# Layer 0 of a four-layer kernel: the softplus of delta moved from VectorE to TensorE and ScalarE

## The chip, the cores and the metric

The kernel runs on one core of a Trainium2 chip, in one launch, all in fp32. The metric is the device time of one execution in microseconds (us). Engines: TensorE (PE; its weight loads are PEld) multiplies matrices into PSUM; VectorE (DVE), ScalarE (ACT) and GpSimd (POOL) work on tiles; SyncE (SP) issues most transfers. Each runs its own instructions in order and waits for the others by semaphores.

## The reference

Input `x` has shape (4, 64, 64, 128): four images of 4096 tokens with 128 channels. Four layers follow one another; the change is in layer 0, a two-dimensional selective scan. Cut to what matters:

```python
xz = x @ w_in                              # x: group-normed; 2 * 256 channels
xc, z = split(xz)
xa = silu(depthwise_conv3x3(xc) + conv_b)
dts, Bp, Cp = split(xa @ w_xproj)          # 8 + 16 + 16
dts = dts @ w_dt                           # 256 channels
delta = softplus(dts + b_dt)
# four scans over the tokens: rows, columns, and both backwards
h = h * exp(delta * A) + (delta * u) * B   # 16 states per channel
y = sum_n(h * C) + u * D
y = layer_norm(y_rows + y_cols + y_rows_back + y_cols_back) * silu(z)
x = x + y @ w_out
```

Layers 1 to 3 (a recurrence in the Fourier domain, an attention with a mixture of experts, and a windowed attention with another) are not touched.

## The kernel before, in words

**The main loop of layer 0** (line 974 on) runs over 512 iterations I: four images b, two halves h of the 256 channels, 64 chunks c of 64 tokens. An iteration has two *half-steps* (kp = 0 and 1). In each, `products` (L850) multiplies on TensorE into two PSUM tiles `db`; VectorE adds the carry (L865) and runs two scans of 128x1024 (L870); GpSimd makes the next carry (L877) and multiplies the result by C (L885); `total` (L905) sums the states of the chunk two iterations earlier on TensorE into `yp`. After the second part of `total`, ScalarE copies `yp` out (L919); there is one `yp`, so the next iteration's `total` waits for these copies. After the first scans of an iteration VectorE makes `du` (L826). ScalarE also computes the *decay* exp(delta * A) of the next four chunks (a quad), four activations per iteration (`decay`, L773), into one of two buffers.

`db` has three buffers of which a half-step takes two. So the first matmuls of the next `products` may run at once, but the rest wait until the first of the two running scans has ended: TensorE can be about half a half-step ahead of VectorE.

**Work beside the loop.** While image b is scanned, the generators `back` of image b - 1, and `front` and `middle` of image b + 1 are advanced at fixed places: one *slot* after `total` in each half-step (lines 1013 and 1026; one more in some iterations with h = 0). A generator runs to its next `yield`, and so its instructions stand in a written order on TensorE, VectorE and ScalarE (`manual_schedule`). Between half-steps TensorE's order is: `products`, `total`, slot work, `products` again. All slot work of these generators shares one PSUM bank, `bg` (`own_bank`, one buffer), so a tile there is released only when its last reader is done.

`middle` prepares the scan's inputs, in eight blocks k of 512 tokens, in the half h = 1 of the image before. It is used for images 1 to 3; image 0 goes through `opening`, which the change leaves alone. One block is a *round* of 14 slots, seven iterations:

- slots 0 to 3: for each half the convolution (L383, 24 instructions), Silu, a transposition (`columns`, L393) and its copy
- slot 4: `projected` (L404) and two copies; slot 5: `turned_b` (L418) and a copy by VectorE
- slot 6: for half 0, `steps` (L426, the product with `w_dt` into `bg`), then ScalarE: Abs (L491), Relu (L492), Exp (L493), Identity with bias 1 (L494), Ln (L496)
- slot 7: for half 0, VectorE sums (L498, L501, L502), and the result is stored (`keep_steps`, L432)
- slots 8 and 9: the same two for half 1
- slots 10 to 13: for each half `columns` and `flipped` (L435), each with a copy (L516) and a store

With u = exp(-|s|) for s = dts + b_dt, and w the rounded 1 + u, softplus is ln(w) - ((w - 1) - u) + relu(s); the middle term gives back what the rounding of 1 + u took. Even slots lie in the first half-step of an iteration, and the decay of that iteration follows them on ScalarE; the `yp` copies come behind the decay. ScalarE's Ln and Exp each need a table load (L496, L773), which the profile shows as ACT_TABLE_LOAD.

The tiles u, r, v and the other 2 KB tiles of the generators come from one pool of ten buffers (`tmp`, "t2k").

Of the kernel before, what the change touches and what calls it, by code (L numbers as in the profile page):

```python
# [8 lines left out]
AF = mybir.ActivationFunctionType  # L9
ALU = mybir.AluOpType  # L10
# [4 lines left out]
P = 128  # L15
# [5 lines left out]
BLK = 512  # L21
# [39 lines left out]
def tl(pool, shape, tag, dtype=F32, bufs=None):  # L61
    return pool.tile(shape, dtype, name=tag, tag=tag, bufs=bufs)
# [99 lines left out]
def layer0(cm, x, W, x1, also, ahead, kept):  # L162


    tc, nc = cm.tc, cm.nc
    wl = kept.enter_context(tc.tile_pool(name="l0k", bufs=1))
    dr = kept.enter_context(tc.tile_pool(name="l0dram", bufs=2, space=DRAM))
    with ExitStack() as ctx:
        ctx.enter_context(nc.allow_non_contiguous_dma(reason="parameters laid over partitions"))
        wp = ctx.enter_context(tc.tile_pool(name="l0w", bufs=1))  # L170
        tmp = ctx.enter_context(tc.tile_pool(name="l0t", bufs=10))
# [66 lines left out]
        for i in range(2):  # L238
            t = tl(wp, [P, QC, 2, NH0, TC], f"dA{i}")
# [16 lines left out]
        for i in range(2):  # L256
            t = tl(wp, [P, 8, PADW], f"padded{i}")
# [108 lines left out]
        def shifted(i, pool, tag, queue=nc.sync):  # L366

            k, h = divmod(i, 2)
            x3 = [tl(pool, [3 * CG, 2, 8 * PADW], tag) for _ in range(2)]
            for dy in range(3):  # L370
                s0 = (8 * k + dy) * PADW
                for i in range(2):
                    queue.dma_start(
                        x3[i][dy * CG : (dy + 1) * CG],
                        xc_d[4 * h + 2 * i : 4 * h + 2 * i + 2, :, s0 : s0 + 8 * PADW]
                        .rearrange("g p s -> p g s"),
                    )
            return x3

        def convolved(ps, h, x3):  # L380
            for dx in range(3):
                for g in range(4):
                    nc.tensor.matmul(  # L383
                        ps[g * CG : (g + 1) * CG, :], lhsT=cdiag[:, 4 * h + g, dx, :],
                        rhs=x3[g // 2][:, g % 2, :].rearrange(
                            "p (r w) -> p r w", w=PADW
                        )[:, :, dx : dx + HW],
                        start=(dx == 0), stop=(dx == 2),
                    )

        def columns(ps, src):
            for i in range(4):
                nc.tensor.transpose(  # L393
                    ps[:, i * P : (i + 1) * P], src[:, i * P : (i + 1) * P], cm.ident
                )

        def keep_turned(b, h, k, t):
            nc.sync.dma_start(
                img[b]["xT"][h, k * BLK : (k + 1) * BLK, :].rearrange("(t p) c -> p t c", p=P), t
            )  # L400

        def projected(ps, xa):
            for h in range(2):
                nc.tensor.matmul(  # L404
                    ps[0:NX, :], lhsT=w_xp[:, h, :], rhs=xa[h], start=(h == 0), stop=(h == 1)
                )

        def keep_c(b, k, xd):
            nc.sync.dma_start(
                img[b]["ct"][8 * k : 8 * k + 8].rearrange("c n t -> n c t"),  # L410
                xd[RANK + NST : NX, :].rearrange("n (c t) -> n c t", t=TC),
            )

        def turned_b(ps, k, xd, xr):
            pb = ps[:, 0 : 8 * NST].rearrange("p (c n) -> p c n", n=NST)
            for c in range(8):
                for j in range(2):
                    nc.tensor.matmul(  # L418
                        pb[j * TC : (j + 1) * TC, c, :],
                        lhsT=xr[0:NX, c, :] if j else xd[0:NX, c * TC : (c + 1) * TC],  # L420
                        rhs=cm.ident[0:NX, RANK : RANK + NST], start=True, stop=True,
                    )
            nc.vector.tensor_copy(BT[:, 8 * k : 8 * k + 8, :], pb)

        def steps(ps, h, xd):
            nc.tensor.matmul(  # L426
                ps, lhsT=w_dt[:, h * P : (h + 1) * P], rhs=xd[0:RANK, :],
                start=True, stop=True,
            )

        def keep_steps(b, h, k, r):
            nc.sync.dma_start(img[b]["dl"][h, :, k * BLK : (k + 1) * BLK], r)  # L432

        def flipped(ps, t):
            nc.tensor.matmul(  # L435
                ps, lhsT=flip, rhs=t.rearrange("p t c -> p (t c)"), start=True, stop=True
            )

        def keep_both(b, h, k, j, t):
            for i in range(2):  # L440
                nc.sync.dma_start(
                    img[b]["dT"][h, 8 * k + i : 8 * k + 8 : 2, j]
                    .rearrange("t r c -> r t c"), t[i * TC : (i + 1) * TC],
                )

        def middle(b, bank, pool, tag, ahead):

            ready = [shifted(i, pool, tag) for i in range(ahead)]
            for k in range(NBLK):
                cols = slice(k * BLK, (k + 1) * BLK)  # L450
                xa = []
                for h in range(2):
                    ps = bank()
                    convolved(ps, h, ready.pop(0))
                    if 2 * k + h + ahead < 2 * NBLK:
                        ready.append(shifted(2 * k + h + ahead, pool, tag))
                    xh = tl(tmp, [P, BLK], "t2k")
                    nc.scalar.activation(xh, ps, AF.Silu, bias=vec[:, 0, h : h + 1])
                    y0 = tl(tmp, [P, BLK], "t2k")
                    nc.scalar.activation(y0, xh, AF.Copy, scale=d4[:, h : h + 1])  # L460
                    nc.sync.dma_start(img[b]["y0"][:, h, cols], y0)
                    xa.append(xh)
                    yield
                    ps = bank()
                    columns(ps, xa[h])
                    t = tl(tmp, [P, 4, P], "t2k")
                    nc.scalar.copy(t, ps.rearrange("p (t c) -> p t c", c=P))
                    keep_turned(b, h, k, t)
                    yield
                ps = bank()  # L470
                projected(ps, xa)
                xd = tl(tmp, [P, BLK], "t2k")
                nc.scalar.copy(xd[0:NX, :], ps[0:NX, :])
                xr = tl(tmp, [P, 8, TC], "t2k")
                nc.scalar.copy(
                    xr[0:NX], ps[0:NX, :].rearrange("p (c t) -> p c t", t=TC)[:, :, ::-1]
                )
                keep_c(b, k, xd)
                yield
                turned_b(bank(), k, xd, xr)  # L480
                rs = []
                for h in range(2):
                    yield


                    ps = bank()
                    steps(ps, h, xd)
                    bias = vec[:, 1, h : h + 1]
                    u = tl(tmp, [P, BLK], "t2k")
                    r = tl(tmp, [P, BLK], "t2k")  # L490
                    nc.scalar.activation(u, ps, AF.Abs, bias=bias)  # L491
                    nc.scalar.activation(r, ps, AF.Relu, bias=bias)  # L492
                    nc.scalar.activation(u, u, AF.Exp, scale=-1.0)  # L493
                    nc.scalar.activation(ps, u, AF.Identity, bias=cm.ones[:, 0:1])  # L494
                    v = tl(tmp, [P, BLK], "t2k")
                    nc.scalar.activation(v, ps, AF.Ln)  # L496
                    yield
                    nc.vector.scalar_tensor_tensor(  # L498
                        ps, ps, 1.0, u, ALU.subtract, ALU.subtract
                    )  # L500
                    nc.vector.tensor_tensor(ps, v, ps, ALU.subtract)  # L501
                    nc.vector.tensor_tensor(r, ps, r, ALU.add)  # L502
                    keep_steps(b, h, k, r)
                    rs.append(r)

                yield
                for h in range(2):
                    t = None
                    for j in range(2):
                        ps = bank()  # L510
                        if j == 0:
                            columns(ps, rs[h])
                        else:
                            flipped(ps, t)
                        t = tl(tmp, [P, 4, P], "t2k")
                        nc.scalar.copy(t, ps.rearrange("p (t c) -> p t c", c=P))  # L516
                        keep_both(b, h, k, j, t)
                        yield
# [215 lines left out]
        def place(I):  # L734
            u, c = divmod(I, NCHUNK)
            return divmod(u, 2) + (c,)
# [237 lines left out]
        with tc.manual_schedule(engines=engines):  # L974
            for I in range(N):
                b, h, c = place(I)
# [19 lines left out]
                w = quads.get(I // QC + 1)  # L996
# [1829 lines left out]
```

## Time and profile before

| what | us |
|---|---|
| runs shown: lowest, median, highest | 10,066.63, 10,080.76, 10,089.57 |
| the profiled execution's own time | 10,065.04 |
| its span, first to last instruction | 10,063.1 |
| main loop of layer 0, about 219 to 5,653 us of the span | 5,434 |
| busy in the span: PE, DVE, ACT, POOL | 8,590.0, 7,471.3, 5,347.1, 5,373.5 |
| of it the scans L870 | 4,571.0 |
| of it GpSimd's product L885 | 4,659.0 |
| three VectorE lines of the softplus in `middle`, 48 times each | 99.0 |

In the profile's lines a group is: line, engine, operation, out<-in with the shapes, xcount, then busy time in us and the mean of one instruction in ns, then the idle time before it and who ended it. Lines of a timeline have the start in us from the span's first instruction, the length, the engine and the line; what stands in brackets is the engine's idle time before, and its releaser. A table by stage gives for each stretch its length, each engine's busy time and number of instructions, the clock granted to TensorE (1.00 is full), the busy share of the DMA engines and GB/s.

### The profile page before, as it was taken

How to read it: one execution, taken by the hardware profiler on the slowest of the kernel's cores; microseconds unless marked ns; L12 is line 12 of the kernel's file. 1: busy time of each engine (PE TensorE's matmuls, PEld its weight loads, DVE VectorE, ACT ScalarE, POOL GpSimd, SP SyncE). 2: the span in 40 equal slices, each digit the busy share in tenths (PEclk: the TensorE clock that was granted, in tenths of full speed). 3: DMA queues.
4: the chain of work that ended last, by engine and by line, in shares of the span. 5: the costliest groups of instructions: out<-in, count | busy, mean ns of one | idle time of the engine just before them, and what ended most of it. 6: DMA issues, size and time to landing. Idle time of an engine off the chain costs nothing.

```text
span 10063.1 us, 193320 instructions
## 1 busy us (share of the span) xinstructions
PE 8590.0 (85%) x73048; PEld 4219.2 (42%) x73048; DVE 7471.3 (74%) x11089; ACT 5347.1 (53%) x13309; POOL 5373.5 (53%) x2788
## 2 busy tenths in 40 slices
PE   7888888889988899988888649999999958888776
PEld 3333444444434444444333334444444435554442
DVE  4999999999999999999999765454551123455656
ACT  5775555775547665556522237767776613443331
POOL 4999999899999899999999500000000000100000
PEclk8899999999999999999999869999999977888887
DMA  7344454445543455444333321111101062212101
GB/s 212 103 132 128 137 141 114 128 130 146 145 126 120 120 160 144 132 120 124 87 103 94 107 66 31 37 38 34 38 18 33 16 223 48 61 45 52 43 24 47
DMA packets 1081627, 957.38 MB, mean 95 GB/s; under 512 B 165356, under 2 KB 825616, under 8 KB 1073920
## 3 DMA queue, kind: packets, MB, share of 16 engines
q1 hardware_dynamic: 1055298, 880.82, 29.7%
q0 software_dynamic: 18560, 63.37, 3.4%
q8 instruction: 586, 9.60, 0.4%
q14 instruction: 337, 2.76, 0.1%
q10 hardware_dynamic: 6846, 0.83, 0.1%
HBM read 608.77 MB, written 335.80 MB: 94 GB/s over the span
## 4 chain that ended last, share of the span: by engine, by line
PE 42%; DVE 26%; POOL 10%; issue 8%; ACT 6%; DMA 5%; SPq 2%; DVEq 0%; ACTq 0%; POOLq 0%
DVE big L870 15%; POOL big L885 8%; PE qk L1758 7%; PE av L1817 7%; PE yp L905 5%; PE db L850 4%; PE x L2607 2%; DVE tex L2613 2%; DVE du L826 2%; PE s L2373 1%; DMA xo<-xT_d 1%; PE po L2398 1%; PE bg L383 1%; DVE mx L2337 1%; PE s L2331 1%
## 5 line engine op out<-in xcount | busy, mean ns | idle before, releaser
L885 POOL TENSOR_TENSOR big<-big,ct 128x2048 f32<-128x2048 f32 x1024 | 4659.0, 4550 | 76.1
L870 DVE TENSOR_TENSOR_SCAN big<-dA,db 128x1024 f32<-128x1024 f32 x2048 | 4571.0, 2273 | 13.6 <-DMA xo<-xT_d 8.6
L850 PE MATMUL db<-dg,du 32*64 32x256 f32 x32768 | 1896.0, 418 | 606.0 <-DVE big L870 466.6
L905 PE MATMUL yp<-big,both 128*64 128x256 f32 x16384 | 2229.3, 419 | 60.5 <-ACT yc L919 47.6
L905 PEld LDWEIGHTS yp<-big,both 128*64 128x64 f32 x16384 | 1191.8, 148 | 1031.0 <-issue 563.6
L850 PEld LDWEIGHTS db<-dg,du 32*64 32x64 f32 x32768 | 653.3, 135 | 1791.9 <-issue 1692.3
L1817 PE MATMUL av<-e,x 128*128 128x512 f32 x2048 | 974.0, 592 | 4.6 <-ACT e L1812 4.6
L1762 ACT ACTIVATE e<-qk,nk 128x512 f32<-128x512 f32 x1024 | 692.6, 685 | 534.1 <-PE qk L1758 533.2
L1758 PE MATMUL qk<-a,xT 128*128 128x512 f32 x2048 | 966.6, 594 | 8.6 <-ACT e L1762 7.9
L919 ACT COPY yr<-yp 128x64 f32<-128x64 f32 x1024 | 221.7, 216 | 1346.9 <-PE yp L905 1331.4
L818 ACT ACTIVATE dg<-mask,BT 128x32 f32<-128x32 f32 x4096 | 896.6, 318 | 10.9 <-PE db L850 8.6
L773 ACT ACTIVATE dA<-dp,A 128x252 f32<-128x252 f32 x2048 | 866.0, 498 | 49.8 <-issue 26.1
L1331 POOL TENSOR_TENSOR g_rs<-g_rs,k_qrow 128x4 f32<-128x4 f32 x32 | 41.0, 1282 | 1499.9 <-DVE g_rs L1330 1499.9
L1758 PEld LDWEIGHTS qk<-a,xT 128*128 128x128 f32 x2048 | 378.0, 190 | 462.3 <-issue 358.0
L1817 PEld LDWEIGHTS av<-e,x 128*128 128x128 f32 x2048 | 381.6, 190 | 434.7 <-issue 393.2
L1812 ACT ACTIVATE e<-e 128x1024 f32<-128x1024 f32 x510 | 538.7, 1056 | 15.4
L877 POOL TENSOR_TENSOR cy<-big,a 128x32 f32<-128x32 f32 x1008 | 365.6, 363 | 299.6 <-DVE big L870 239.3
L2380 ACT ACTIVATE e<-s 128x576 f32<-128x576 f32 x448 | 272.7, 647 | 398.8 <-PE s L2373 396.2
L2112 POOL TENSOR_TENSOR ln_rs<-ln_rs,mroot 128x4 f32<-128x4 f32 x64 | 64.8, 1012 | 756.0 <-DVE ln_rs L2111 501.6
L2392 POOL COPY vp<-vt 112x80 f32<-112x80 f32 x112 | 30.2, 270 | 781.2 <-PE po L2398 755.3
L2613 DVE SCALAR_TENSOR_TENSOR tex<-x,gw,tex 128x128 f32<-128x128 f32 x768 | 264.5, 344 | 198.0 <-PE x L2607 184.3
L826 DVE TENSOR_TENSOR du<-xo,dt 128x256 f32<-128x256 f32 x512 | 387.7, 757 | 0.0
(569 smaller groups left out, 9805.6 us busy)
## 6 DMA issues: line engine op xcount, KB each, us to landing
ct<-ct_d SPq DMA_DIRECT2D x1024, 128.0 KB
xo<-xT_d SPq DMA_DIRECT2D x2048, 32.0 KB
dg_d<-dg SPq DMA_DIRECT2D x256, 256.0 KB
dg<-dg_d SPq DMA_DIRECT2D x256, 256.0 KB
t4k<-xc_d SPq DMA_DIRECT2D x288, 132.0 KB
dp<-dl_d SPq DMA_DIRECT2D x256, 128.0 KB
dT_d<-t2k SPq DMA_DIRECT2D x256, 128.0 KB
dt<-dT_d SPq DMA_DIRECT2D x512, 64.0 KB
```

The costliest lines, as they stand in the source:

```text
L773: nc.scalar.activation(w["dA"][:, :, g, n, 1:], w["dp"][:, g, :, 1:], AF.Exp, scale=A[:, w["h"], g, n : n + 1],)
L818: nc.scalar.activation(q["dg"][:, n, :], mask, AF.Copy, scale=BT[:, q["c"], n : n + 1])
L826: nc.vector.tensor_tensor(q["du"], q["xo"], q["dt"].unsqueeze(1).to_broadcast([P, 2, P]), ALU.mult)
L850: nc.tensor.matmul(bs[j][p * TC : (p + 1) * TC, g * NH0 : (g + 1) * NH0, t0 : t0 + QR], lhsT=q["du"][rows, kp, g * TC : (g + 1) * TC], rhs ...
L870: nc.vector.tensor_tensor_scan(st[:, u].rearrange("p n t -> p (n t)"), q["w"]["dA"][:, c % QC].rearrange("p g n t -> p (g n t)"), bs[j].re ...
L885: nc.gpsimd.tensor_tensor(sv, sv, q["ct"].rearrange("p n t -> p (n t)").unsqueeze(1) .to_broadcast([P, 4, NH0 * TC]), ALU.mult,)
L905: nc.tensor.matmul(yp[p * TC : (p + 1) * TC], lhsT=both, rhs=st[:, :, p * NH0 + n, :], start=(n == 0), stop=(n == NH0 - 1),)
L1758: nc.tensor.matmul(ps, lhsT=me["xT"][:, kt * P : (kt + 1) * P], rhs=me["a"][k], start=True, stop=True,)
L1762: nc.scalar.activation(e[:, j, :], ps, AF.Exp, bias=me["nk"][:, kt : kt + 1], scale=2.0)
L1812: nc.scalar.activation(es[g + 2], es[g + 2], AF.Exp)
L1817: nc.tensor.matmul(avs[b, k], lhsT=img[b]["x"][:, kt, :], rhs=e[:, j, :], start=(kt == 0), stop=(kt == NT - 1),)
L2613: nc.vector.scalar_tensor_tensor(t[:, i, :], s[:, e * D : (e + 1) * D], gw[:, j, 4 * a + e : 4 * a + e + 1], t[:, i, :], ALU.mult, ALU.add,)
```

## The change

In `middle`, slots 6 to 9 are put in another order and another form. Slots 6 and 7 now hold `steps` and ScalarE's work for half 0 and half 1; the Identity writes an SBUF tile w, and after Ln a further Identity turns w into 1 - w. So each half has four parts v = ln(w), w = 1 - w, u and r, whose sum is the softplus. Slots 8 and 9 hold the sums: four products with the identity matrix accumulate in `bg`, and ScalarE copies the bank to r, which is stored as before. The number of slots stays 14.

```diff
                 turned_b(bank(), k, xd, xr)
+                parts = []
+                for h in range(2):
+                    yield
+                    ps = bank()
+                    steps(ps, h, xd)
+                    bias = vec[:, 1, h : h + 1]
+                    u, r, w, v = [tl(tmp, [P, BLK], "t2k") for _ in range(4)]
+                    nc.scalar.activation(u, ps, AF.Abs, bias=bias)
+                    nc.scalar.activation(r, ps, AF.Relu, bias=bias)
+                    nc.scalar.activation(u, u, AF.Exp, scale=-1.0)
+                    nc.scalar.activation(w, u, AF.Identity, bias=cm.ones[:, 0:1])
+                    nc.scalar.activation(v, w, AF.Ln)
+                    nc.scalar.activation(w, w, AF.Identity, scale=-1.0, bias=cm.ones[:, 0:1])
+                    parts.append((v, w, u, r))
                 rs = []
                 for h in range(2):
                     yield
                     ps = bank()
-                    steps(ps, h, xd)
-                    bias = vec[:, 1, h : h + 1]
-                    u = tl(tmp, [P, BLK], "t2k")
-                    r = tl(tmp, [P, BLK], "t2k")
-                    nc.scalar.activation(u, ps, AF.Abs, bias=bias)
-                    nc.scalar.activation(r, ps, AF.Relu, bias=bias)
-                    nc.scalar.activation(u, u, AF.Exp, scale=-1.0)
-                    nc.scalar.activation(ps, u, AF.Identity, bias=cm.ones[:, 0:1])
-                    v = tl(tmp, [P, BLK], "t2k")
-                    nc.scalar.activation(v, ps, AF.Ln)
-                    yield
-                    nc.vector.scalar_tensor_tensor(
-                        ps, ps, 1.0, u, ALU.subtract, ALU.subtract
-                    )
-                    nc.vector.tensor_tensor(ps, v, ps, ALU.subtract)
-                    nc.vector.tensor_tensor(r, ps, r, ALU.add)
+                    for i, t in enumerate(parts[h]):
+                        nc.tensor.matmul(
+                            ps, lhsT=cm.ident, rhs=t, start=(i == 0), stop=(i == 3)
+                        )
+                    r = parts[h][3]
+                    nc.scalar.copy(r, ps)
                     keep_steps(b, h, k, r)
                     rs.append(r)
```

More of the change, by code (lines that the diff above doesn't have):

```diff
@@ L480, in middle @@
                 turned_b(bank(), k, xd, xr)
-                rs = []
+                parts = []
                 for h in range(2):
@@ L493, in middle @@
                     nc.scalar.activation(u, u, AF.Exp, scale=-1.0)
-                    nc.scalar.activation(ps, u, AF.Identity, bias=cm.ones[:, 0:1])
-                    v = tl(tmp, [P, BLK], "t2k")
-                    nc.scalar.activation(v, ps, AF.Ln)
-                    yield
-                    nc.vector.scalar_tensor_tensor(
-                        ps, ps, 1.0, u, ALU.subtract, ALU.subtract
-                    )
-                    nc.vector.tensor_tensor(ps, v, ps, ALU.subtract)
-                    nc.vector.tensor_tensor(r, ps, r, ALU.add)
+                    nc.scalar.activation(w, u, AF.Identity, bias=cm.ones[:, 0:1])
+                    nc.scalar.activation(v, w, AF.Ln)
+                    nc.scalar.activation(w, w, AF.Identity, scale=-1.0, bias=cm.ones[:, 0:1])
+                    parts.append((v, w, u, r))
+                rs = []
+                for h in range(2):
+                    yield
+                    ps = bank()
[5 more added lines that the diff above has]
+                    nc.scalar.copy(r, ps)
                     keep_steps(b, h, k, r)
```

## The prediction

> **What bounds the kernel now.** I read the page first, then the table by stage, then the groups of the loop, then the timelines of one round on TensorE, VectorE and ScalarE. The page's header and first part:
>
> ```profile
> span 10063.1 us, 193320 instructions
> PE 8590.0 (85%) x73048; PEld 4219.2 (42%) x73048; DVE 7471.3 (74%) x11089; ACT 5347.1 (53%) x13309; POOL 5373.5 (53%) x2788
> ```
>
> An average over four layers says little. Of the table by stage, the second half (h = 1) of the pass over image 1, in which `middle` of image 2 runs:
>
> ```profile
> core 0: us, PE busy (x) PEld busy (x) DVE busy (x) ACT busy (x) POOL busy (x), PEclk, DMA share, GB/s
> 2266.00:2950.00 684.00, 620.98 (x7024) 279.39 (x7020) 665.40 (x628) 347.77 (x810) 635.80 (x298) 0.93 0.52 139
> ```
>
> VectorE is busy 665.4 of 684 us (97%), and GpSimd 93%; TensorE is at 91%. VectorE sets the pace, but TensorE is close behind. What the edit takes from VectorE, and the ScalarE line it changes, stand in the groups of the loop:
>
> ```profile
> L501 DVE TENSOR_TENSOR bg<-t2k,bg 128x512 f32<-128x512 f32 x48 | 33.4, 696 | 1.6
> L494 ACT ACTIVATE bg<-t2k,ones 128x512 f32<-128x512 f32 x48 | 33.2, 692 | 1.6
> L502 DVE TENSOR_TENSOR t2k<-bg,t2k 128x512 f32<-128x512 f32 x48 | 33.2, 691 | 1.6
> L498 DVE SCALAR_TENSOR_TENSOR bg<-bg,t2k 128x512 f32<-128x512 f32 x48 | 32.4, 674 | 0.0
> ```
>
> TensorE's timeline over slots 5 to 9 of one round (start, length, line; xN counts instructions):
>
> ```profile
> 1008.70 1.12 PE L426 MATMUL bg<-t2k,w_dt 8*128 8x512 f32 x2
> 1009.75 1.91 PE L850 MATMUL db<-dg,du 32*64 32x256 f32 x32
> 1011.59 1.95 PE L905 MATMUL yp<-big,both 128*64 128x256 f32 x16
> 1013.47 0.66 PE L850 MATMUL db<-dg,du 32*64 32x256 f32 x8
> 1015.28 1.45 PE L850 MATMUL db<-dg,du 32*64 32x256 f32 x24 [1.15 <-DVE big L870]
> 1018.05 3.48 PE L905 MATMUL yp<-big,both 128*64 128x256 f32 x16 [1.32 <-ACT yc L919]
> ```
>
> Here one 512-column fp32 product is two instructions and takes 1009.75 - 1008.70 = 1.05 us until the next starts. An undisturbed `total` part takes 1.88 us (1011.59 to 1013.47), undisturbed `products` 1.46 us (1022.52 to 1023.98 later in this view). So a half-step costs TensorE 3.34 us before any slot work. And TensorE stands still twice while VectorE works on the softplus: the reader is to see the 1.32 us wait for ScalarE's copies of `yp`. After it `total` takes 3.48 us instead of 1.95. Two stretches of the same place show why (columns as above):
>
> ```profile
> 1014.40:1017.80 3.40, 1.35 (x24) 0.48 (x24) 3.40 (x3) 3.39 (x10) 3.32 (x3) 1.00 0.41 110
> 1017.80:1021.20 3.40, 3.15 (x16) 1.90 (x16) 3.33 (x6) 0.11 (x1) 3.40 (x1) 0.50 0.19 49
> ```
>
> TensorE was busy 1.35 of 3.4 us; the next 3.4 us were granted half the clock. VectorE's timeline over the two lumps of this round:
>
> ```profile
> 1012.85 4.46 DVE L870 TENSOR_TENSOR_SCAN big<-dA,db 128x1024 f32<-128x1024 f32 x2
> 1017.23 0.67 DVE L498 SCALAR_TENSOR_TENSOR bg<-bg,t2k 128x512 f32<-128x512 f32 x1
> ...
> 1019.48 4.46 DVE L870 TENSOR_TENSOR_SCAN big<-dA,db 128x1024 f32<-128x1024 f32 x2
> ...
> 1024.39 4.46 DVE L870 TENSOR_TENSOR_SCAN big<-dA,db 128x1024 f32<-128x1024 f32 x2
> ...
> 1031.09 4.46 DVE L870 TENSOR_TENSOR_SCAN big<-dA,db 128x1024 f32<-128x1024 f32 x2
> ```
>
> Between a lump's scan and the next, 6.6 to 6.7 us pass; the one in between took 4.91.
>
> **The change part by part.** Three images times eight blocks times two halves are 48 softplus blocks, 24 rounds.
>
> *Removed from VectorE:* 0.674 + 0.696 + 0.691 = 2.06 us per block, 48 x 2.06 = 98.9 us, all in a stage that VectorE bounds. That is the most that can be gained.
>
> *Added to ScalarE:* an Identity from SBUF to SBUF per block. The like is L493 (629 ns); in the timeline such activations start 0.57 to 0.66 us apart, so 0.60 us. The first Identity now writes SBUF; no price difference that matters (692 against 629 ns). The copy out of PSUM is like L516, 586 ns, and stands alone in slots 8 and 9. The table loads stay at four per round: Ln and the decay's Exp, once per block as now.
>
> *Added to TensorE:* four 512-column fp32 products with the 128x128 identity per block, eight instructions, 384 in all. Each pair of instructions of L435 and L354 starts 0.53 us apart, of long runs such as L1758 0.429 us, and the last to the next work takes 0.52 us. I take one start at 0.53, the next seven instructions at 0.43, and 0.09 at the end: 3.63 us per sum. The ends: 8 x 0.429 = 3.43, and 8 x 0.533 + 0.09 = 4.36 if no weight load is ever hidden.
>
> *Moved:* the `steps` product and ScalarE parts of half 1, from slot 8 to slot 7; both stores of delta, from slots 7 and 9 to 8 and 9.
>
> *Where this ends up on the path.* Follow a round from the start A of the first Abs (1009.86 above). Today, the mean over the 24 rounds (read from the timelines): `total` after the first lump starts at A + 8.20, the scan after the second lump (1031.09 above) at A + 22.13, the one after it at A + 27.19. The `total` waits for ScalarE, which works through the activations, the decay's table load and four exponentials, and only then the `yp` copies; queued behind the new Identity they all end 0.60 later. Nothing hides it: so A + 8.80. Slot 7's `steps` product (1.05 us) comes before, in the 1.15 us that TensorE waits at 1014.1: free. From there TensorE has no pause: total 1.88, sum 3.63, products 1.46, total 1.88, sum 3.63, products 1.46 = 13.94, and 0.40 from there to the scan (1023.98 to 1024.39): A + 23.14. VectorE, without its lumps, could have had that scan at about A + 18: it stands waiting for `products` in both half-steps, about 2.8 and 2.2 us. Then a scan 4.91 later, as in rounds now: A + 28.05, against 27.19. The lookahead is restored by then (slots 10 to 13 hold 0.6 and 1.05 us), so the round is 0.86 us longer: 24 x 0.86 = +20.6 us. The 2 x 2.06 us taken from VectorE are thus in it: they return as waits for TensorE.
>
> *The clock.* In 20 of the 24 rounds today it falls to half in slots 7 to 8. With the edit the pause before `total` is 1016.7 to 1018.65, 1.9 us, with 0.1 us before it: within a 3.4 us stretch TensorE is busy 1.4 to 2.3 us, as in the stretch shown. If it falls, 3.4 us at half rate cost 1.7 us of a path that is now TensorE's alone. Today's falls are already in the mean 22.13. I take 18 of 24 rounds: +30.6 us; ends 0 and, falling twice per round, 81.6.
>
> The Trainium skill ("TensorE: Matmul & The Clock Gate", Why this matters for your kernels) tells to avoid idle gaps over about 3 us; by it a gap of 1.9 us would not lower the clock, and the sum would be +20.6 us. The stretch shown has no gap over 1.4 us, and half the clock follows; the row decides.
>
> *Other waits.* The first sum needs the bank that half 1's Relu reads last: that Relu ends about A + 9.9 (copies to 8.55, then Abs and Relu), TensorE gets there at A + 10.68. Slot 8's copy makes ScalarE wait for the sum; behind it are the decay and the next `yp` copies, ready at about A + 18.2, while TensorE wants them at A + 22.7. SP's queue holds half 1's store until that copy lands, around A + 22, where today it waits for L502 at A + 21; behind it are the fetches for two iterations ahead (20 us). GpSimd issues none of the moved transfers; it has 7% to spare and follows the scans. A tile pool of ten buffers now gives 20 tiles per round instead of 18: each buffer's last reader is at least six slots back. In every fourth round the decay that ends 0.60 later is the last before a new quad's scan; that scan has the 2.8 us of waiting behind it. All these at nothing; if the covers fail, each costs under 1 us per round, 24 us.
>
> *Sum:* 20.6 + 30.6 = +51 us. The profiled execution took 10,065.0 us (span 10,063.1 and 1.9 around it), so 10,116 on its scale; it lies 15.7 below the median of the runs, 10,080.8, on which I put the forecast: **10,132 us**.
>
> **The rivals.**
> 1. *The clock stays up* (0.18): TensorE's new work fills the stretches. For it: after `total` nothing pauses. Against: the pause before is as long as today's. 10,080.8 + 20.6 = 10,101.
> 2. *The sums are dearer* (0.16): every identity load is exposed, as within the pairs of L354 and L435. 2 x (4.36 - 3.63) x 24 = 35 us more: 10,167. Against it: L1758 reloads 128x128 weights for every instruction and starts them 0.429 us apart.
> 3. *Faster: the sums hide and VectorE keeps the whole gain* (0.11): place, slots 8 and 9; price, -98.9 us, 9,982. It needs a sum to fit beside 3.34 us in a half-step of about 5.05, under 1.7 us. For it: the 24 instructions of the convolution take 2.78 us, four at a time; against: those use 32 columns each, these all 128, and the lower end is 3.43.
>
> **How the numbers follow.** My forecast has 0.50, rivals 0.18, 0.16 and 0.11, and 0.05 is for something unnamed. The likeliest case alone reaches 10,100 to 10,155. The range 10,075 to 10,180 holds the forecast and rivals 1 and 2, 0.84, and the ends of the prices: all low 3.43 and no fall, +11; all high and a fall in each round, +97. Rival 3 is left out. What this kernel's measurement can tell from no change is about 0.2%, 20 us. Rival 1 lies on that edge, so: slower 0.74, same 0.14, faster 0.12.
>
> **What would show it.** Right: the three VectorE groups are gone (busy time about 99 us less), 384 new matmuls on `bg` starting 0.43 to 0.53 us apart, VectorE's waits for `products` in the second halves of images 0 to 2 up by about 5 us per round, `total`'s wait for ScalarE's copies near 1.9 us in each round, and rounds some 2 us longer. Wrong: scans after slots 8 and 9 coming 5 us apart; or a granted clock of 1.0 there; or sums off 3.4 to 4.4 us. What would upset it most is a reordering of transfers elsewhere in layer 0, which this trace can't show.

## The result and the profile after

The changed kernel takes 10,144.15 us (median of 4 runs, 10,139.64 to 10,161.23) against 10,073.69 us for the kernel before in the same comparison (4 runs); the ratio is 1.0079 with a 95% interval of 1.0067 to 1.0092. It is 0.8% slower; the forecast was 10,132 us, put on a median of 10,080.8 us before, which was 10,073.69 in this comparison: +51 us was forecast, and the medians lie 70 us apart. The profiled execution took 10,142.51 us against 10,065.04: 77.5 us more. The page's header and first part after:

```profile
span 10140.5 us, 194052 instructions
PE 8719.0 (86%) x73432; PEld 4271.0 (42%) x73432; DVE 7389.4 (73%) x10945; ACT 5406.7 (53%) x13405; POOL 5371.9 (53%) x2788
```

VectorE is busy 81.9 us less (7,471.3 to 7,389.4), with 144 instructions fewer: the 99 us of the three groups are gone, but `du`, for one, takes 8.9 us more (387.7 to 396.6); TensorE is busy 129 us more, with 384 instructions more. The kernel got slower although the engine that set its pace has less to do. The table by stage for the half h = 1 of image 1, the stage shown before:

```profile
2300.20:3005.50 705.30, 658.40 (x7158) 296.09 (x7156) 639.53 (x581) 368.55 (x843) 636.68 (x299) 0.96 0.49 135
```

It lasts 705.3 us instead of 684.7; VectorE's share falls from 97% to 91%, TensorE's rises from 91% to 93%. The three halves that hold `middle` are 28.2, 20.6 and 25.1 us longer (boundaries at the first scan of each half), 73.9 of the 77.5 us; the rest of layer 0 and the other layers differ by a few microseconds of both signs. New and changed groups of the loop:

```profile
L502 PE MATMUL bg<-t2k,ident 128*128 128x512 f32 x384 | 188.3, 635 | 0.0
L493 ACT ACTIVATE t2k<-t2k,ones 128x512 f32<-128x512 f32 x48 | 34.7, 723 | 1.6
L495 ACT ACTIVATE t2k<-t2k,ones 128x512 f32<-128x512 f32 x48 | 34.6, 722 | 1.6
```

The sums (L502) are there, 48 x 8 instructions, and an Identity from SBUF to SBUF takes 723 ns. TensorE's timeline through slots 7 to 9 of one round:

```profile
1019.22 1.12 PE L426 MATMUL bg<-t2k,w_dt 8*128 8x512 f32 x2
1020.27 2.25 PE L854 MATMUL db<-dg,du 32*64 32x256 f32 x32
1024.62 3.68 PE L909 MATMUL yp<-big,both 128*64 128x256 f32 x16 [2.10 <-ACT yc L923]
1028.23 4.13 PE L502 MATMUL bg<-t2k,ident 128*128 128x512 f32 x8
1032.30 0.69 PE L854 MATMUL db<-dg,du 32*64 32x256 f32 x16
...
1033.76 1.95 PE L909 MATMUL yp<-big,both 128*64 128x256 f32 x16
1035.63 3.70 PE L502 MATMUL bg<-t2k,ident 128*128 128x512 f32 x8
1039.26 0.69 PE L854 MATMUL db<-dg,du 32*64 32x256 f32 x16
```

From 1024.62 on TensorE has no pause worth the name until 1039.26. An undisturbed sum takes 1039.26 - 1035.63 = 3.63 us; the first one of this round takes 4.07 because it begins at half the clock, and the `total` ahead of it 3.61 instead of 1.88. VectorE's timeline of the same stretch shows who pays:

```profile
1023.17 4.46 DVE L874 TENSOR_TENSOR_SCAN big<-dA,db 128x1024 f32<-128x1024 f32 x2
1027.55 0.76 DVE L830 TENSOR_TENSOR du<-xo,dt 128x256 f32<-128x256 f32 x1
1033.93 0.29 DVE L869 TENSOR_TENSOR db<-db,cy 128x16 f32<-128x16 f32 x2 [5.62 <-PE db L854]
1034.14 4.46 DVE L874 TENSOR_TENSOR_SCAN big<-dA,db 128x1024 f32<-128x1024 f32 x2
1040.89 0.29 DVE L869 TENSOR_TENSOR db<-db,cy 128x16 f32<-128x16 f32 x2 [2.29 <-PE db L854]
```

VectorE stands 5.62 and 2.29 us waiting for `products`, where it had two lumps of 2.06 us. Over all rounds, from 3 to 33 us after the first Abs, VectorE's waits for `products` rise from 0.8 to 7.0 us per round, and they are 167 of its 174 us of waiting there. The two stretches that hold the pause before `total` and what follows (stretch, its length, each engine's busy time with its instructions, the granted clock, DMA share, GB/s):

```profile
1021.20:1024.60 3.40, 1.22 (x24) 0.28 (x20) 3.40 (x4) 3.39 (x11) 3.32 (x3) 0.66 0.27 77
1024.60:1028.00 3.40, 3.38 (x16) 1.90 (x16) 3.40 (x3) 3.35 (x5) 3.40 (x2) 0.50 0.37 111
```

The mean of 0.66 puts the fall at about 1022.3 us, shortly before the pause begins (`products` ends at 1020.27 + 2.25 = 1022.52), and half the clock lasts through the pause, through `total` and into the first sum (0.83 over the next 3.40 us). Read over all 24 rounds, from the scans of a round's first slot to those 14 slots later, a round is 78.1 us long against 75.0 before, 24 x 3.1 = 74 us; the loss is in the rounds, as forecast, and it is half again as large as forecast. The experiments ask two things: whether the sums' time on TensorE is what counts, or the order of the parts and ScalarE's longer chain; and what the clock's share is.

### The profile page after: what moved, and what is told of

The parts are those of the page before. It is cut to its first block, busy times and chain, and to the rows that moved or that the text cites. A ratio compares the mean times of both kernels' runs of the same rounds, so it can differ in the third digit from the quotient of the medians.

```text
span 10140.5 us, 194052 instructions
## 1 busy us (share of the span) xinstructions
PE 8719.0 (86%) x73432; PEld 4271.0 (42%) x73432; DVE 7389.4 (73%) x10945; ACT 5406.7 (53%) x13405; POOL 5371.9 (53%) x2788
## 4 chain that ended last, share of the span: by engine, by line
PE 46%; DVE 26%; issue 9%; ACT 6%; DMA 5%; POOL 5%; SPq 2%; DVEq 0%; ACTq 0%; POOLq 0%
DVE big L874 15%; PE qk L1762 7%; PE av L1821 7%; PE yp L909 7%; PE db L854 5%; POOL big L889 4%; PE x L2611 2%; DVE tex L2617 2%; DVE du L830 2%; PE bg L502 2%; PE s L2377 1%; PE bg L383 1%; PE po L2402 1%; DVE db L869 1%; PE s L2335 1%
## 5 line engine op out<-in xcount | busy, mean ns | idle before, releaser
L854 PE MATMUL db<-dg,du 32*64 32x256 f32 x32768 | 1863.3, 414 | 562.2 <-DVE big L874 422.4
L854 PEld LDWEIGHTS db<-dg,du 32*64 32x64 f32 x32768 | 645.5, 133 | 1737.1 <-issue 1640.5
L2384 ACT ACTIVATE e<-s 128x576 f32<-128x576 f32 x448 | 272.4, 647 | 399.2 <-PE s L2377 396.6
L869 DVE TENSOR_TENSOR db<-db,cy 128x16 f32<-128x16 f32 x2016 | 256.1, 171 | 226.5 <-PE db L854 222.7
```

The lines of the kernel that those rows point to most:

```text
L854: nc.tensor.matmul(bs[j][p * TC : (p + 1) * TC, g * NH0 : (g + 1) * NH0, t0 : t0 + QR], lhsT=q["du"][rows, kp, g * TC : (g + 1) * TC], rhs ...
```

## The experiments

Each was timed against the kernel before on the same chip; ratios are to it, with their 95% intervals. The changed kernel stands at 1.0079. "A" is again the start of a round's first Abs, and a round is 14 slots.

### Half of each sum

```diff
-                    for i, t in enumerate(parts[h]):
+                    for i, t in enumerate((parts[h][0], parts[h][3])):
...
-                            ps, lhsT=cm.ident, rhs=t, start=(i == 0), stop=(i == 3)
+                            ps, lhsT=cm.ident, rhs=t, start=(i == 0), stop=(i == 1)
```

> The changed kernel with two of the four products per sum (v and r); it leaves out the term (1 - w) + u that gives back the rounding of 1 + u. ScalarE's work is unchanged. Theory (in slots 8 and 9 the path is TensorE's, so every product there counts in full): each sum takes 1.9 instead of 3.63 us, the round is 2 x 1.73 = 3.5 us shorter, 78.1 to about 74.7, the kernel about 83 us faster than the changed one: 10,060 +- 15, within 0.2% of before. Rival (ScalarE's longer chain and the wait of `total` for the `yp` copies set the time): no more than 10 us gained, about 10,135.

Measured: 10,053.38 us, ratio 0.9984 (0.9975 to 0.9994), a round of 74.5 us. Four products fewer per round take 3.6 us off it (78.1 to 74.5), where the theory said 3.5. ScalarE's chain, the wait of `total` and the falling clock are all still there: from A + 3 to A + 22 a round has 5.26 us at half the clock, as in the changed kernel. (The sums here leave out the term that gives back the rounding of 1 + u.) So the products of the sums count in full, one for one. The rival, with 10 us at most, is out.

### The same order with VectorE adding, in SBUF

```diff
-                    ps = bank()
-                    for i, t in enumerate(parts[h]):
-                        nc.tensor.matmul(
-                            ps, lhsT=cm.ident, rhs=t, start=(i == 0), stop=(i == 3)
-                        )
-                    r = parts[h][3]
-                    nc.scalar.copy(r, ps)
+                    v, w, u, r = parts[h]
+                    nc.vector.tensor_tensor(v, v, w, ALU.add)
+                    nc.vector.tensor_tensor(v, v, u, ALU.add)
+                    nc.vector.tensor_tensor(r, v, r, ALU.add)
```

> The changed kernel's order (both halves' parts in slots 6 and 7, with both Identities on ScalarE), but in slots 8 and 9 the four parts are added by three VectorE additions in SBUF, no sum on TensorE and no copy. Theory (the loss is the sums on TensorE and the clock, not the order): VectorE's lumps of 2.07 us lie after the scans of slots 8 and 9 as before, TensorE has 3.3 us of work there and keeps ahead even at half the clock; the scan after slot 10 comes at about A + 27.3 against 27.2 before: 10,075 +- 15, within 0.2% of before. Rival (the order itself, two ScalarE chains one after the other, costs the time): 10,120 or more.

Measured: 10,273.67 us, ratio 1.0203 (1.0186 to 1.0220). Taken at its word the expectation would give this to the rival. But the run's own profile shows something neither had: the groups of the three additions,

```profile
L503 DVE TENSOR_TENSOR t2k<-t2k 128x512 f32<-128x512 f32 x48 | 138.9, 2894 | 1.6
L502 DVE TENSOR_TENSOR t2k<-t2k 128x512 f32<-128x512 f32 x48 | 108.9, 2269 | 1.6
L501 DVE TENSOR_TENSOR t2k<-t2k 128x512 f32<-128x512 f32 x48 | 33.8, 705 | 0.0
```

and one of them in the timeline, with GpSimd's product beside it:

```profile
1047.70 0.69 DVE L502 TENSOR_TENSOR t2k<-t2k 128x512 f32<-128x512 f32 x1
1047.87 4.89 POOL L886 TENSOR_TENSOR big<-big,ct 128x2048 f32<-128x2048 f32 x1
1048.43 4.89 DVE L503 TENSOR_TENSOR t2k<-t2k 128x512 f32<-128x512 f32 x1
```

An addition that takes 0.69 us by itself takes 4.89 when it starts during GpSimd's product, and ends shortly after it. Of the 144 additions 43 started during such a product; these 43 alone were slow, and each ended 0.55 us after the product. The three groups cost 281.6 us of VectorE instead of 99. The run therefore says nothing on the order; the experiment had changed two things, the order and where VectorE's inputs lie. (In the kernel before, each of the three operations has one input in PSUM and takes 0.67 to 0.70 us beside the same product: 122 of the 144 started during one.) The Trainium skill ("GPSIMD Engine Reference", Specifications) has the row for it: GpSimd's SBUF interfaces are shared with VectorE, and two SBUF inputs contend. This run agrees and gives the price, up to a whole GpSimd instruction.

### The same order with VectorE adding, one input in PSUM

```diff
                     nc.scalar.activation(v, w, AF.Ln)
-                    nc.scalar.activation(w, w, AF.Identity, scale=-1.0, bias=cm.ones[:, 0:1])
-                    parts.append((v, w, u, r))
+                    parts.append((v, u, r))
...
                     ps = bank()
-                    for i, t in enumerate(parts[h]):
-                        nc.tensor.matmul(
-                            ps, lhsT=cm.ident, rhs=t, start=(i == 0), stop=(i == 3)
-                        )
-                    r = parts[h][3]
-                    nc.scalar.copy(r, ps)
+                    v, u, r = parts[h]
+                    nc.scalar.activation(ps, u, AF.Identity, bias=cm.ones[:, 0:1])
+                    nc.vector.scalar_tensor_tensor(
+                        ps, ps, 1.0, u, ALU.subtract, ALU.subtract
+                    )
+                    nc.vector.tensor_tensor(ps, v, ps, ALU.subtract)
+                    nc.vector.tensor_tensor(r, ps, r, ALU.add)
```

> The order of the changed kernel with the sums on VectorE as in the kernel before, one operand in PSUM: slots 6 and 7 make v, u and r of both halves; in slots 8 and 9 ScalarE's Identity writes 1 + u into the bank and VectorE makes its three operations of before. It differs from the run with three additions in SBUF, where an addition with both inputs in SBUF took 4.9 us beside GpSimd's product. Theory (neither the order nor VectorE made that run slow, but the two SBUF inputs): VectorE's lumps are 2.06 us again, the scan after slot 10 at about A + 27.5 against 27.2 before: 10,080 +- 15, within 0.2% of before. Rival (two ScalarE chains one after the other hold up slots 8 and 9): 10,120 or more.

Measured: 10,081.85 us, ratio 1.0016 (1.0006 to 1.0025), a round of 75.7 us against 75.0. Within the 0.2% expected. Both halves' parts first costs about 0.7 us per round, some 16 us, and not 80. So of the changed kernel's loss the greater part is not the order. The run says nothing on ScalarE's longer chain: it has no second Identity in slots 6 and 7, and `total` starts at A + 8.23, against 8.20 in the kernel before.

### `steps` three times, to fill the pause

```diff
                     ps = bank()
-                    steps(ps, h, xd)
+                    for _ in range(3 if h else 1):
+                        steps(ps, h, xd)
```

> The changed kernel with slot 7's `steps` product of half 1 issued three times into the same bank (the last one counts): 48 more products, 1.05 us each, in the time in which TensorE waits for the copies of `yp` anyway. `products` then ends about A + 8.2 and `total` still starts at A + 8.9, so the pause before it shrinks from 2.0 to 0.7 us. Theory (the pause lowers the clock, and that costs 2.0 us per round on a path that is TensorE's alone): the granted clock stays at 1.00 in slots 7 and 8, the round falls from 78.1 to about 76.1 us, the kernel to about 10,097 us, +0.2 to +0.3% against before. Rival (the clock is incidental, the sums and ScalarE's wait explain the whole loss): no change, 10,140 to 10,150, although the clock is up.

Measured: 10,150.23 us, ratio 1.0075 (1.0058 to 1.0092): no change against the changed kernel. But the clock was not up. The stretches around the pause in one round (columns as in the table by stage):

```profile
1017.90:1021.30 3.40, 3.21 (x35) 0.75 (x33) 2.25 (x2) 3.37 (x11) 3.32 (x3) 0.73 0.29 91
1021.30:1024.70 3.40, 2.99 (x14) 1.91 (x16) 3.38 (x4) 3.35 (x8) 3.40 (x1) 0.50 0.23 67
```

TensorE was busy 3.21 of 3.40 us in the first stretch, and the clock fell within it, at about 1019.4 us; it fell in all 24 rounds (5.12 us at half the clock per round, against 5.26). In the 3.41 us ahead of these falls TensorE was busy 3.11 us in the mean. Busy time alone does not hold the clock. The extra products use 8 rows (`xd[0:RANK]`, shown as 8x512), and that suggested the next run. On the price of the clock this run says nothing.

### Two full-array products in the same place

```diff
                     ps = bank()
+                    for _ in range(2 if h else 0):
+                        nc.tensor.matmul(
+                            ps, lhsT=cm.ident, rhs=parts[0][3], start=True, stop=True
+                        )
                     steps(ps, h, xd)
```

> The changed kernel with two products of the full 128x128 identity and r of half 0 put ahead of slot 7's `steps` of half 1, into the same bank, where `steps` then overwrites them: 2.1 us of work over all 128 rows of the array, in the time in which TensorE would wait for the `yp` copies. The run with `steps` three times had the same amount of busy time there, but over 8 rows, and the clock fell all the same in slots 7 and 8. Theory (what keeps the clock up is work over the whole array, and half the clock costs 2.0 us per round): the clock stays at 1.00 there in most rounds, the round falls from 78.1 to about 76.1, the kernel to about 10,095, +0.2 to +0.3% against before. Rival (falls have another cause, or cost nothing that ends up on the path): no change, about 10,145.

Measured: 10,103.55 us, ratio 1.0039 (1.0026 to 1.0051), a round of 76.4 us. The same stretches of one round, and TensorE's timeline:

```profile
1017.90:1021.30 3.40, 2.34 (x38) 1.50 (x32) 2.64 (x5) 3.37 (x11) 3.32 (x3) 1.00 0.26 66
1021.30:1024.70 3.40, 3.40 (x12) 1.44 (x8) 2.58 (x3) 3.26 (x4) 3.12 (x5) 1.00 0.37 106
```

```profile
1014.28 1.98 PE L488 MATMUL bg<-t2k,ident 128*128 128x512 f32 x4
1016.20 1.12 PE L426 MATMUL bg<-t2k,w_dt 8*128 8x512 f32 x2
...
1019.68 1.95 PE L913 MATMUL yp<-big,both 128*64 128x256 f32 x16 [0.91 <-ACT yc L927]
1021.56 3.70 PE L506 MATMUL bg<-t2k,ident 128*128 128x512 f32 x8
1025.19 0.69 PE L858 MATMUL db<-dg,du 32*64 32x256 f32 x16
```

Less busy time in the stretch (2.34 us) than with `steps` three times, and the clock stays at 1.00; it fell in 6 of 24 rounds. `total` takes 1.88 us and the sum 3.63 again. 48 added products make the changed kernel about 40 us faster (1.0079 to 1.0039): the clock's share of the loss is about that at the least, 1.7 us per round. The theory said 2.0 for all rounds, and the rounds without a fall show it: there the scan behind the second sum, at A + 25.26 in the changed kernel, comes at A + 23.22 in the mean; in the 6 with a fall it comes at A + 24.97.

### The sums on TensorE, one half at a time

In slots 6 and 7 half 0, in slots 8 and 9 half 1, four parts each:

```diff
-                parts = []
+                rs = []
                 for h in range(2):
                     yield
...
-                    parts.append((v, w, u, r))
-                rs = []
-                for h in range(2):
                     yield
                     ps = bank()
-                    for i, t in enumerate(parts[h]):
+                    for i, t in enumerate((v, w, u, r)):
...
-                    r = parts[h][3]
                     nc.scalar.copy(r, ps)
```

> The sums on TensorE as in the changed kernel, but one half at a time as in the kernel before: parts of half 0 in slot 6, its sum in slot 7, half 1 in slots 8 and 9. Theory (what counts is TensorE's work and its pauses): the sum of slot 7 waits for ScalarE's chain (about A + 5.3, TensorE there at A + 3.6), but it fills the time in which TensorE would wait for the `yp` copies; `total` of slot 8 starts about A + 12.3, the scan after slot 10 at about A + 29 against 30.2 in the changed kernel: 10,100 +- 25, faster than the changed kernel by 20 to 70 us and slower than before by 10 to 50. Rival (both halves' parts first is what keeps the loss small, since the parts are then ready): slower than the changed kernel, over 10,160.

Measured: 10,094.05 us, ratio 1.0021 (1.0012 to 1.0031), a round of 75.6 us. TensorE's timeline:

```profile
1015.59 1.95 PE L905 MATMUL yp<-big,both 128*64 128x256 f32 x16
1018.39 3.70 PE L499 MATMUL bg<-t2k,ident 128*128 128x512 f32 x8 [0.85 <-ACT t2k L494]
1022.02 0.69 PE L850 MATMUL db<-dg,du 32*64 32x256 f32 x16
1022.86 0.69 PE L850 MATMUL db<-dg,du 32*64 32x256 f32 x16 [0.15 <-issue]
1023.48 1.95 PE L905 MATMUL yp<-big,both 128*64 128x256 f32 x16
```

The sum begins 0.85 us late, waiting for Ln and the second Identity, but there is no wait for the `yp` copies behind it, and the clock fell in one of 24 rounds. So "both first" made the parts ready early, as the rival says, and lost more by it than it gained: it leaves the old pause in slot 7 and puts 7.26 us of sums behind it. Most of what this order wins is the clock's: the scan after slot 10 comes at A + 27.70 here, at A + 30.17 in the changed kernel, and at A + 28.13 in the 18 rounds of the preceding run whose clock stayed up.

### The order of before with less of both

Ln takes 1 + u by its own bias and writes PSUM; VectorE adds once, and the term that gives back the rounding of 1 + u is left out:

```diff
-                    nc.scalar.activation(ps, u, AF.Identity, bias=cm.ones[:, 0:1])
-                    v = tl(tmp, [P, BLK], "t2k")
-                    nc.scalar.activation(v, ps, AF.Ln)
+                    nc.scalar.activation(ps, u, AF.Ln, bias=cm.ones[:, 0:1])
                     yield
-                    nc.vector.scalar_tensor_tensor(
-                        ps, ps, 1.0, u, ALU.subtract, ALU.subtract
-                    )
-                    nc.vector.tensor_tensor(ps, v, ps, ALU.subtract)
                     nc.vector.tensor_tensor(r, ps, r, ALU.add)
```

> The order of the kernel before, with less of both: Ln takes 1 + u by its own bias of 1 and writes PSUM, and VectorE adds r in one operation (one input in PSUM); it leaves out the term that gives back the rounding of 1 + u. Theory (the loop is VectorE's as long as TensorE keeps ahead): each lump is 0.69 instead of 2.06 us, so 2 x 1.37 us per round and 66 us in all; TensorE's work is as before: 10,006 +- 15, 0.5 to 0.8% faster than before. Rival (TensorE's half clock, not VectorE, sets these half-steps): less than 30 us gained.

Measured: 10,003.68 us, ratio 0.9939 (0.9922 to 0.9956), a round of 72.0 us, against the 10,006 expected. As long as TensorE keeps ahead, VectorE's time taken away here is gained nearly in full: 0.61%, 61 us (44 to 79 by the interval) of the 66. ScalarE's chain is shorter here too (`total` at A + 7.65 instead of 8.20) and the clock falls less (3.27 us per round instead of 7.9), so a part may be theirs; the rival, under 30 us, is out either way. Taking work from VectorE was worth something; its price on TensorE was the fault.

### Two parts on TensorE, one half at a time

```diff
-                    nc.scalar.activation(ps, u, AF.Identity, bias=cm.ones[:, 0:1])
-                    v = tl(tmp, [P, BLK], "t2k")
-                    nc.scalar.activation(v, ps, AF.Ln)
+                    nc.scalar.activation(u, u, AF.Ln, bias=cm.ones[:, 0:1])
                     yield
-                    nc.vector.scalar_tensor_tensor(
-                        ps, ps, 1.0, u, ALU.subtract, ALU.subtract
-                    )
-                    nc.vector.tensor_tensor(ps, v, ps, ALU.subtract)
-                    nc.vector.tensor_tensor(r, ps, r, ALU.add)
+                    ps = bank()
+                    for i, t in enumerate((u, r)):
+                        nc.tensor.matmul(
+                            ps, lhsT=cm.ident, rhs=t, start=(i == 0), stop=(i == 1)
+                        )
+                    nc.scalar.copy(r, ps)
```

> The sums on TensorE, one half at a time as in the earlier run of that order, but of two parts, with ScalarE's chain cut to Abs, Relu, Exp and Ln with its own bias of 1; it leaves out the term that gives back the rounding of 1 + u. No VectorE work. Theory (a sum is free as long as it fits the room that TensorE has in a half-step, 1.7 us, or a pause that it has anyway): the parts of half 0 are ready at A + 3.9, TensorE is there at A + 3.6, the sum takes 1.9 us and fills the pause before the `yp` copies (A + 7.5); the scan after slot 10 at about A + 18 to 19 and nearly all of VectorE's 99 us is gained: 9,985 +- 20, 0.7 to 1.1% faster than before. Rival (any product added to these slots delays the scans): 10,030 or more.

Measured: 9,961.02 us, ratio 0.9894 (0.9878 to 0.9911), a round of 71.2 us. This beats both kernels, by 1.1% and 1.8%, but like the preceding run it leaves out the term that gives back the rounding of 1 + u. TensorE's timeline from slot 7 on:

```profile
1009.12 1.95 PE L903 MATMUL yp<-big,both 128*64 128x256 f32 x16
1011.26 1.99 PE L497 MATMUL bg<-t2k,ident 128*128 128x512 f32 x4 [0.19 <-ACT t2k L493]
1013.17 0.69 PE L848 MATMUL db<-dg,du 32*64 32x256 f32 x16
...
1014.98 1.95 PE L903 MATMUL yp<-big,both 128*64 128x256 f32 x16 [0.28 <-POOL big L883]
```

A sum of 1.91 us fits where TensorE used to stand still; the clock fell in no round, and the scans that follow (1015.02, 1020.22, 1025.72 on VectorE) are 5.2 and 5.5 us apart. The 24 x 3.8 us of shorter rounds are 91 of the 102 us between the medians. VectorE's waits for `products` in the half h = 1 of image 0 are down to 6.6 us, where the changed kernel has 60.7.

## Why the prediction was right, point by point

*What bounds the kernel, and what is removed.* Right. VectorE's 98.9 us are gone from its instructions, though its busy time fell by 81.9 only, and where TensorE kept ahead a cut was gained (one addition instead of three operations: about 61 of 66 us).

*The sums.* Right to the last digit that was given: the second sum of a round takes 3.63 us in the mean (the first, which half the clock can reach, 4.08). That they are on the path in full is shown by the halved sums, 3.6 us per round for four products.

*ScalarE's chain.* Right but for 0.1 us. `total` starts at A + 8.90 in the mean; forecast A + 8.80. It starts 0.70 us later than in the kernel before (8.20), not 0.60: the row taken for the second Identity (Exp without a bias tile, 629 ns) was a little too cheap; an Identity from SBUF to SBUF takes 723 ns. That is 0.1 us per round, 2.4 us.

*The path.* 13.94 us from `total` to the last `products` at full clock. What stands in the place of "a scan 4.91 later, A + 28.05" is A + 30.17 in the mean. Put together from the measured terms, 8.90 + 13.94 + 0.40 + 4.91 = 28.15, which leaves 2.02 us per round for the clock. The 18 rounds with full clock of the run with two full-array products have that scan at A + 28.13, so the path of the prediction is shown by itself.

*The clock.* This is the term that was mis-sized. "I take 18 of 24 rounds: +30.6 us": the clock fell in all 24, for 5.26 us per round from A + 3 to A + 22, that is for one or two intervals of 3.41 us, and it cost 2.02 x 24 = 48 us. Two full-array products in slot 7 took back about 40 of them. The kernel before has more half clock there, 7.9 us per round, and VectorE waits for `products` only 0.8 us per round all the same (7.0 in the changed kernel): what changed is that the path there is TensorE's. The reason given, that the pause before `total` leaves TensorE too little busy time in 3.4 us, was incomplete. In 5 of the 24 rounds, the one shown among them, the clock fell before that pause began, with TensorE busy 2.96 to 3.22 of the 3.41 us ahead of the fall; and with `steps` three times in the pause the clock fell in every round. What makes it fall stays open.

*The sum.* 20.6 + 30.6 = 51 us forecast; of the 77.5 us measured between the profiled executions, 74 lie in the rounds: 24 x 0.96 = 23 us for the path at full clock, 48 for the clock, and the rest after slot 10. The result lies in the range, and even in the 10,100 to 10,155 of the likeliest case, but the forecast number is nearer to it than the sum deserves: of the 20 to 26 us that were missing in the sum, 7 were made up by the higher median on which it stood.

*The rivals.* The clock staying up (20.6 us slower): it did not; where two full-array products held it up in 18 of 24 rounds, the kernel was 0.39% slower than before, about 40 us, and a quarter of the rounds still had a fall. The Trainium skill's rule to leave no idle gap over about 3 us ("TensorE: Matmul & The Clock Gate", Why this matters for your kernels) doesn't agree with these runs. The clock fell in all 24 rounds of the changed kernel, and in 22 of them TensorE had stood still no longer than 2.0 us at a time in the 6.8 us ahead of the fall (3.05 us in the other two). Dearer sums: wrong, 3.63 us where the clock is full. The sums hidden: wrong with four parts and right with two, whose 1.91 us are near the 1.7 us that the prediction gave as the room.

*Other waits at nothing.* No run tests them singly. What VectorE waits for in the rounds is `products` (PE db L854) almost alone, and the rounds' 74 us leave them little. Of the signs that were named, `total`'s wait was 1.7 us in the mean and absent in 3 rounds (1.9 in each was named), and the waits for `products` rose by 6.2 us per round (5 were named).

## What to carry to other kernels

Before work is moved off the engine that sets the pace, ask of the engine that takes it how long a single piece may be between two deliveries: here TensorE was idle 9% of the stage before, but a half-step had room for only 1.7 us, and sums of 3.63 us made VectorE wait 6.2 us more per round, 2.0 of it the clock's, where it was spared 4.1 us of work. A piece is free if it fits that room or fills a pause that is there anyway; so look for the pause, and put the work into it rather than behind it. And an experiment that swaps engines should keep each operand's memory, or it measures that as well.

## What the hardware showed that was not expected

- What holds TensorE's clock is not the busy share in the profile. With two more 8-row products in the pause it fell to half in 24 of 24 rounds (busy 2.15 to 3.41 of the 3.41 us ahead of the fall); with two 128-row products in their place it fell in 6 of 24, and stayed up in the round shown, with 2.34 of 3.40 us busy. That the number of rows is the cause is suggested by these two runs and not isolated.
- A VectorE addition with both inputs in SBUF took 0.69 us alone and up to 5.31 us when it started during GpSimd's product of 4.5 us; the operations of the kernel before, with one input in PSUM, took 0.67 to 0.70 us beside the same product.
